# A four-layer GNN kernel: in layer 0, edge features transposed an iteration ahead, and the weighted rows' sums moved

## The chip, the cores and the metric

The kernel runs on one core of one Trainium2 chip, in one launch. The metric is the device time of that launch in microseconds, as the median of several runs. Below, PE is the matrix engine (TensorE), DVE the vector engine, ACT the scalar engine, POOL the GpSimd engine (here it issues the gathers), SP the engine that issues the other DMAs. Each engine works its queue strictly in order, and an instruction that needs another engine's result waits on a semaphore.

## What is computed

Four layers of a graph network over N = 12,500 nodes of 128 values and E = 212,500 directed edges, sorted by their destination. Each layer normalises the node rows, applies a ReLU, sends them through a message step of its own kind, and adds the result to the node rows. The change touches layer 0 alone, an attention layer with edge features (16 values an edge, 4 heads of 32 values), whose reference is

```
Wh = (h @ W.T).reshape(N, H, D)
Wh_src = Wh[src]
Wh_dst = Wh[dst]
attn = (jnp.concatenate([Wh_src, Wh_dst], axis=-1) * a[None]).sum(-1)
attn = jax.nn.leaky_relu(attn, negative_slope=0.2)
attn = attn + edge_feat @ W_e.T
max_v = jax.ops.segment_max(attn, dst, num_segments=N)
...
exp_v = jnp.exp(attn - max_v[dst])
denom = jax.ops.segment_sum(exp_v, dst, num_segments=N)
alpha = exp_v / (denom[dst] + 1e-09)
agg = jax.ops.segment_sum(alpha[..., None] * Wh_src, dst, num_segments=N)
out = agg.reshape(N, H * D)
return _layer_norm(jax.nn.gelu(out, approximate=False), ln_scale, ln_bias)
```

So each edge needs the row of its source node (a gather from device memory), a logit for each head, a softmax over the edges that share a destination, and a sum of the weighted rows for each destination.

## The kernel before

**Tiling.** The edges are cut into NG = 208 groups of 1,024 (T = 8 tiles of 128 edges, one edge a partition). Nodes are worked on in NK = 25 blocks of 512 (`node0`). Since edges are sorted by destination, a group touches only a window of W = 128 destinations, whose place is read from a table into a register. The loop of layer 0 runs over the groups as a software pipeline: in iteration g the logits of group g are made, the softmax of groups of four (SG = 4) follows in steps (`weights`), and the rows of group g - 7 (LAG = 7) are weighted and summed. The transposed sums gather in one large SBUF array, `acc`.

**Order.** The whole block stands under a manual schedule: instructions go into each engine's queue in the order in which the Python code issues them, and the tile framework adds the semaphore waits. A tile has a number of buffers (2 unless `bufs` says otherwise); a new one waits until the last reader of the one that had its place is done.

**One iteration g, in the order of issue.**

- `nodes.step(g)`: one step of each node block under way. A block ends layer 0 for 512 nodes: PE transposes `acc` (L553), ACT a Gelu (L557), DVE norms (L507 to L516, L564 to L566), stores.
- `slots.step(g % 2)`, and again `slots.step()` later: steps of `Slots`, which builds tables for layers 1 and 3 beside this loop (large DVE operations L889 to L971, runs of 20 matmuls L892 and L958).
- `load(g + 2)`: SP issues the loads of `ef` (edge features, 256 KB for four groups, every fourth iteration, 2 buffers), `rb` (256 KB, L1019) and `sdw` (L1023).
- `logits(g)`, first part: POOL issues eight gathers of 128 rows into an X buffer (L730; there are LAG + 8 = 15 X buffers). PE transposes the edge features into the PSUM tile `pt` (L1032, 2 buffers), ACT copies that to `eT` (L1034), PE multiplies it with the edge weights (`pew`, L1036). DVE builds the one-hot `ST` (L1038) and PE multiplies it with `sdw`, eight matmuls (`psd`, L1041). `pew` and `psd` lie in the same tile `pt`.
- `hot(g + 1 - LAG)`: ACT builds the float one-hot S of a later reader (L1102, eight L1105, L1106).
- the second part of `weights`, if one is under way.
- `add_up(g - LAG - 1)`: DVE adds the PSUM tile `pag` (one buffer) to `acc` at the window's place (L1120).
- `spread_out(g - LAG)`: DVE multiplies the gathered rows by alpha into `msg` (L1112, 2 buffers; it is the last reader of X, so that it gives an X buffer back), and PE sums them with eight float32 matmuls, which are 16 instructions, into `pag` (L1116).
- `slots.step()`, the last part of `weights`, and the first part of the next one in every fourth iteration (its loads L1056 and L1058, DVE L1061 to L1074, ACT L1075).
- `logits(g)`, second part: DVE makes `at` from `psd`, X and `pew` (L1044 to L1047), and SP stores it (L1049) for `weights`.

After the loop the last groups are summed in a tail with one `nodes.step` a group.

Of the kernel before, what the change touches and what calls it, by code (L numbers as in the profile page):

```python
# [14 lines left out]
F = mybir.dt.float32  # L15
# [11 lines left out]
P = 128  # L27
T = 8
GE = P * T
W = 128  # L30
H = 4
# [9 lines left out]
LAG = 7  # L41
# [52 lines left out]
def gnn_kernel(ctx: ExitStack, tc, x, src, dst, ef16, ef9, ew, W0, We0, a0, lns, lnb, W1, b1,  # L94
# [6 lines left out]
    NG = NF + (tail > 0)  # L101
# [15 lines left out]
    vec, act, pool, pe = nc.vector, nc.scalar, nc.gpsimd, nc.tensor  # L117
# [36 lines left out]
    def load_rows(t, d, b0, nb):  # L154
        for b, n, r in rows(b0, nb):
            if r < P:
                pool.memset(t[:, b - b0, :], 0.0)
            nc.sync.dma_start(
                t[:r, b - b0 : b - b0 + n, :],
                d[b * P : b * P + (n - 1) * P + r, :].rearrange("(j p) d -> p j d", p=r))  # L160
# [9 lines left out]
    ident = cst.tile([P, P], F, name="ident")  # L170
# [21 lines left out]
    def bcast(v, name):  # L192
# [11 lines left out]
    sp, pp = (pre.enter_context(p) for p in (tc.tile_pool(name="p0", bufs=3),  # L204
                                             tc.tile_pool(name="p0p", bufs=2, space=PSUM)))
# [27 lines left out]
    for k in range(NK):  # L233
# [16 lines left out]
        pt = pp.tile([P, nb, P], F, name="pt")  # L250
# [275 lines left out]
    def cols(k, j=0, n=NBK):  # L526

        c = k * NBK * P if acc.ring is None else k * NBK * P % acc.ring
        return slice(c + j * P, c + min(j + n, NB - k * NBK) * P)

    def settle(k):

        if acc.ring is not None and k and k * NBK * P % acc.ring == 0:
            a = acc.t
            vec.tensor_tensor(a[..., :W], a[..., :W], a[..., acc.ring :], ALU.add)
            vec.memset(a[..., acc.ring :], 0.0)
# [9 lines left out]
    def node0(sp, pp, k):  # L546
        b0, nb = k * NBK, min(NBK, NB - k * NBK)
        xv = sp.tile([P, nb, D], F, name="xv")
        load_rows(xv, x, b0, nb)
        settle(k)  # L550
        pa = pp.tile([P, nb, P], F, name="pa")
        for j in range(nb):
            pe.transpose(pa[:, j, :], acc.t[:, cols(k, j, 1)], ident)  # L553
        yield
        vec.memset(acc.t[:, cols(k)], 0.0)
        o = sp.tile([P, nb, D], F, name="o")
        act.activation(o, pa, AF.Gelu)  # L557
        yield
        for n in norm(sp, o, nb, None):
            if n is None:  # L560
                yield
            else:
                o = n
        vec.tensor_tensor(o, o, lns_b[:, None, :].to_broadcast([P, nb, D]), ALU.mult)  # L564
        vec.tensor_tensor(o, o, lnb_b[:, None, :].to_broadcast([P, nb, D]), ALU.add)
        vec.tensor_tensor(xv, xv, o, ALU.add)  # L566
        yield from keep(sp, 0, k, xv)
# [424 lines left out]
    with (tc.tile_pool(name="e0", bufs=2) as sp, tc.tile_pool(name="e0p", bufs=2, space=PSUM) as pp,  # L992
# [16 lines left out]
        vec.memset(cut_s[:, :, L:], 0.0)  # L1009
        flat = lambda t: t.rearrange("p h k -> p (h k)")  # L1010
        breg, areg = Window(SP, True), Window(DVE, True)
        loads, xs, alphas, hots = {}, {}, {}, {}
        feats = feature_stream(ef16f, 16, 4, "ef", sp)

        def load(g):

            e = feats(g)
            rb = sp.tile([P, T, P], B16, name="rb", bufs=3)
            nc.sync.dma_start(rb.rearrange("p t q -> p (t q)"),  # L1019
                              rel16[g * T : (g + 1) * T, :].rearrange("t q -> (t q)")[None, :].to_broadcast([P, GE]))  # L1020
            sdw = sp.tile([P, 3 * H], B16, name="sdw", bufs=4)
            n0 = breg.load(bi[0:1, g : g + 1])
            breg.end(nc.sync.dma_start(sdw, sdt[ds(n0, W), :]))  # L1023
            loads[g] = e, rb, sdw

        def logits(g):

            e, rb, sdw = loads.pop(g)
            X = xs[g] = sp.tile([P, T, P + H], F, name="X", bufs=LAG + 8)
            gather(X, tab0, si[:, g, :])  # L1030
            pt = pp.tile([P, P + T * H + T * 3 * H], F, name="pt")
            pe.transpose(pt[:, :P], e, ident)  # L1032
            eT = sp.tile([P, P], F, name="eT")
            act.copy(eT, pt[:, :P])  # L1034
            pew = pt[:, P : P + T * H]
            pe.matmul(pew, eT, WeB, start=True, stop=True)  # L1036
            ST = sp.tile([P, T, P], B16, name="ST")
            vec.tensor_scalar(ST, rb, pcol, None, op0=ALU.is_equal)  # L1038
            psd = pt[:, P + T * H :].rearrange("p (t k h) -> p t k h", k=3, h=H)
            for t in range(T):  # L1040
                pe.matmul(psd[:, t].rearrange("p k h -> p (k h)"), ST[:, t, :], sdw, start=True, stop=True)  # L1041
            yield
            at = sp.tile([P, T, H], F, name="at")
            vec.tensor_reduce(at, psd.rearrange("p t k h -> p t h k"), AX.X, ALU.add)  # L1044
            vec.tensor_tensor(at, at, X[:, :, P:], ALU.add)
            vec.scalar_tensor_tensor(at, at, 0.2, at, op0=ALU.mult, op1=ALU.max)
            vec.tensor_tensor(at, at, pew.rearrange("p (t h) -> p t h", h=H), ALU.add)  # L1047
            a0_ = PADF + g * GE
            nc.sync.dma_start(lgt[a0_ : a0_ + GE, :].rearrange("(p t) h -> p t h", t=T), at)  # L1049
# [49 lines left out]
        def hot(g):  # L1099

            far = sp.tile([P, T], F, name="far")
            act.mul(far, rel[:, g, :], -1.0)  # L1102
            S = hots[g] = sp.tile([P, T, W], F, name="oh")
            for t in range(T):
                act.activation(S[:, t, :], iop, AF.Abs, bias=far[:, t : t + 1])  # L1105
            act.activation(S, S, AF.Relu, bias=ones[:, :1], scale=-1.0)  # L1106

        def spread_out(g):

            X, ev, S = xs.pop(g), alphas.pop(g), hots.pop(g)  # L1110
            msg = sp.tile([P, T, P], F, name="msg")
            vec.tensor_tensor(msg.rearrange("p t (h d) -> p t h d", h=H),  # L1112
                              X[:, :, :P].rearrange("p t (h d) -> p t h d", h=H),
                              ev[:, :, :, None].to_broadcast([P, T, H, HD]), ALU.mult)
            for t in range(T):
                pe.matmul(pag, msg[:, t, :], S[:, t, :], start=t == 0, stop=t == T - 1)  # L1116

        def add_up(g):
            win = ds(areg.load(bir[0:1, g : g + 1], RW - 1), W)
            areg.end(vec.tensor_tensor(acc.t[:, win], acc.t[:, win], pag, ALU.add))  # L1120

        with tc.manual_schedule():
            load(0)
            load(1)
            work = []
            nodes = Nodes(lambda k: node0(ns, np_, k), LAG + 2)
            for g in range(NG + 1):
                nodes.step(g)
                slots.step(g % 2)
                if g + 2 < NG:  # L1130
                    load(g + 2)
                now = None
                if g < NG:
                    now = logits(g)
                    next(now)
                if g + 1 >= LAG:
                    hot(g + 1 - LAG)
                for w in work:
                    next(w)
                if g > LAG:  # L1140
                    add_up(g - LAG - 1)
                if g >= LAG:
                    spread_out(g - LAG)
                slots.step()
                for w in work:
                    next(w, None)
                work = []
                if g and g % SG == 0:
                    work = [weights(g // SG - 1)]
                    next(work[0])  # L1150
                    if g == NG:
                        next(work[0])
                        next(work[0], None)
                        work = [weights(NSG)]
                        next(work[0])
                if now is not None:
                    next(now, None)

            next(work[0])
            for k in range(NG - LAG + 1, NG):  # L1160
                nodes.step(k + LAG)
                if k + 1 < NG:
                    hot(k + 1)
                else:
                    next(work[0], None)
                add_up(k - 1)
                spread_out(k)
            add_up(NG - 1)
            while nodes.step(NG + LAG + 2):
                pass  # L1170
            slots.close()
# [89 lines left out]
    with (tc.tile_pool(name="t1", bufs=1) as tp, tc.tile_pool(name="e1", bufs=3) as sp,  # L1261
# [10 lines left out]
        S, pags, X, here, there = {}, {}, {}, [], []  # L1272
# [5 lines left out]
        with tc.manual_schedule():  # L1278
            g = -1
# [120 lines left out]
    with (tc.tile_pool(name="e2", bufs=3) as sp, tc.tile_pool(name="e2p", bufs=2, space=PSUM) as pp,  # L1400
          tc.tile_pool(name="n2", bufs=2) as ns, tc.tile_pool(name="n2p", bufs=1, space=PSUM) as np_):
        acc.t = sp.tile([P, 3, RW + W], F, name="acc2", bufs=1)
        rows2, mix, _, window2 = layer2(sp, pp, 11, True)
        nodes = Nodes(lambda k: node2(ns, np_, k), 4)
# [6 lines left out]
        with tc.manual_schedule():  # L1411
            vec.memset(acc.t, 0.0)
            mixed[0] = mix(0)
            g = -1
# [121 lines left out]
    with tc.tile_pool(name="l3", bufs=1) as lp:  # L1536
        acc.t, acc.ring = lp.tile([P, AW], F, name="acc3"), None
        stats = lp.tile([P, NK, 6], F, name="stats")
        with (tc.tile_pool(name="t3", bufs=1) as tp, tc.tile_pool(name="e3", bufs=2) as sp,
# [15 lines left out]
            X, S, sums, flat3, going = {}, {}, {}, {}, []  # L1555
# [3 lines left out]
            with tc.manual_schedule():  # L1559
# [4 lines left out]
                g, count, nk, alive = -1, 0, 0, True  # L1564
# [65 lines left out]
    with tc.If(coarse > W - 1):  # L1630
# [154 lines left out]
        with tc.tile_pool(name="es2", bufs=1) as sp, tc.tile_pool(name="es2p", bufs=1, space=PSUM) as pp:  # L1785
            _, _, stream2, window2 = layer2(sp, pp)
# [34 lines left out]
```

## Time and profile before

| | |
|---|---|
| time, median of 12 runs | 9865.54 us (9840.95 to 9888.52) |
| the profiled execution's own time | 9878.95 us |
| its span | 9877.2 us |
| granted clock of PE, mean | 0.708 of full speed |
| PE matmul, busy | 5212.4 us (53%) |
| PE weight loads, busy | 3250.0 us (33%) |
| DVE, busy | 5347.9 us (54%) |
| ACT, busy | 2817.2 us (29%) |
| POOL, busy | 5138.6 us (52%) |
| first L1034 and 208th L1034 (layer 0's loop) | 175.8 and 3303.1 us |
| last L1120 (end of layer 0's tail) | 3361.28 us |

The busy times are those of the whole launch; the span is cut into 40 slices for a course in time, and layer 0's loop covers about the first 13 of them. In the costliest groups of instructions a row reads: line, engine, operation, tile out <- tiles in, count; busy us in all, mean ns of one; then how long the engine stood idle just before such an instruction, and what it was waiting for. "remote" is a release that the trace can't put down to one instruction, "issue" time in which the engine waited for nothing that the profile shows. In the timeline a row reads: start, duration, engine, line, operation, tiles, count, and in brackets the idle time before it. The ends of PE's instructions are modelled, so that a matmul's recorded end and the moment at which another engine gets its result can differ.

From 500 to 3250 us, which is 184 groups, with rows for each shape:

| DVE instruction | busy us, mean ns | idle before it, us |
|---|---|---|
| L1120, addition of `pag` to `acc`, x184 | 52.8, 287 | 251.7 |
| L1044, first instruction of `at`, x184 | 46.3, 252 | 216.2 |
| L1112, `msg`, x184 | 223.4, 1214 | 17.1 |
| L1038, `ST`, x183 | 88.6, 484 | 0.0 |

### The profile page before, as it was taken

To read this page: it belongs to the slowest core of one execution; us is meant where nothing else is said; L and a number is where in the kernel's file an instruction comes from. 1 tells how busy PE (TensorE), PEld (TensorE's weight loads), DVE (VectorE), ACT (ScalarE), POOL (GpSimd) and SP (SyncE) were. 2 spreads that over 40 slices of the span, in tenths; PEclk is the share of its full clock that TensorE was granted. 3 is DMA by queue.
4 is the path that set the end of the run, shared out by engine and by line. 5 is a ranking of instruction groups with operands and counts; after the bars stand their busy time and mean duration, and the time that the engine had idled before them with its cause. 6 is when DMAs were issued, how large, how long until landed. Compare 5 with 4: busy or idle time off the path is not lost. (4 is left out here: it accounts for less than half of the span.)

```text
span 9877.2 us, 105557 instructions
## 1 busy us (share of the span) xinstructions
PE 5212.4 (53%) x33167; PEld 3250.0 (33%) x33168; DVE 5347.9 (54%) x10302; ACT 2817.2 (29%) x7509; POOL 5138.6 (52%) x5434
## 2 busy tenths in 40 slices
PE   2233333333333247778783555555555546666766
PEld 2233333333333225555551333333333321111212
DVE  4466666656666413333343777777777753333333
ACT  2133333333333213333331222222222212333333
POOL 2555555555544265555525555555555535555552
PEclk6555565655655568888886777777777767777777
DMA  7222232222322312222221111111111122222223
GB/s 103 65 74 74 74 75 76 72 72 74 77 72 73 72 54 72 70 73 70 75 56 46 48 54 51 52 51 53 50 51 52 46 87 77 78 78 79 79 78 95
DMA packets 740839, 673.64 MB, mean 68 GB/s; under 512 B 340899, under 2 KB 629014, under 8 KB 740247
## 3 DMA queue, kind: packets, MB, share of 16 engines
q0 software_dynamic: 186624, 382.17, 14.7%
q1 hardware_dynamic: 553643, 284.63, 11.4%
q8 instruction: 263, 4.31, 0.2%
q14 instruction: 309, 2.53, 0.1%
HBM read 603.91 MB, written 63.28 MB: 68 GB/s over the span
## 5 line engine op out<-in xcount | busy, mean ns | idle before, releaser
L730 POOL DMA_INDIRECT X<-tab,si x1664 | 1616.2, 971 | 1451.4 <-DVE msg L1112 677.8
L730 POOL DMA_INDIRECT X<-htab,si x1664 | 1575.7, 947 | 1124.3 <-ACT prods L1350 558.3
L738 POOL DMA_INDIRECT xg<-tab,si x968 | 920.2, 951 | 809.4 <-PE pg L1600 427.9
L738 POOL DMA_INDIRECT X<-htab,si x968 | 937.7, 969 | 697.0 <-PE pag L1309 317.7
L1372 PE MATMUL pag<-prods,oh 128*128 128x352 f32 x3328 | 1244.6, 536 | 0.0
L1116 PE MATMUL pag<-oh,msg 128*128 128x128 f32 x3328 | 721.0, 404 | 328.5 <-DVE msg L1112 283.3
L1372 PEld LDWEIGHTS pag<-prods,oh 128*128 128x128 f32 x3328 | 742.8, 229 | 415.4 <-issue 186.0
L1510 ACT CAST xb<-px 128x384 bf16<-128x384 f32 x1050 | 497.8, 479 | 1147.2 <-PE px L1499 605.6
L1116 PEld LDWEIGHTS pag<-oh,msg 128*128 128x128 f32 x3328 | 668.6, 307 | 343.9 <-DVE msg L1112 286.3
L1337 PE MATMUL py<-mixer,eT 72*128 72x120 f32 x416 | 130.8, 407 | 1212.4 <-ACT eT L1336 1051.5
L1246 ACT ACTIVATE xs<-px,wslot 128x128 f32<-128x128 f32 x1050 | 373.9, 367 | 1223.4 <-PE px L1234 577.6
L1036 PE MATMUL pt<-WeB,eT 128*128 128x32 f32 x416 | 123.2, 387 | 1114.1 <-ACT eT L1034 826.1
L1374 ACT COPY R<-pag 128x352 f32<-128x352 f32 x208 | 94.1, 452 | 1935.0 <-remote 1314.3
L1309 PE MATMUL pag<-oh,X 128*128 128x128 f32 x1936 | 464.3, 331 | 305.0 <-issue 151.0
L1600 PE MATMUL pg<-xg,oh 128*128 128x385 bf16 x968 | 395.9, 420 | 426.1 <-DVE f L1593 351.8
L1234 PE MATMUL px<-tabS,oha 128*32 128x128 f32 x8652 | 529.4, 321 | 165.2 <-ACT xs L1246 88.1
L1215 PE MATMUL pw<-ohb,xs 128*128 128x128 f32 x2100 | 591.6, 369 | 15.9 <-ACT xs L1246 14.1
L745 DVE TENSOR_TENSOR oh<-iop,rel 128x1024 f32<-128x1024 f32 (+1 forms) x321 | 389.5, 1214 | 316.5 <-PE pm L1609 101.6
L1499 PE MATMUL px<-tabS,oha 128*32 128x384 bf16 x4326 | 452.5, 405 | 120.6 <-issue 101.1
L1350 ACT ACTIVATE prods<-X,ef 128x128 f32<-128x128 f32 x1664 | 509.8, 392 | 12.4 <-DMA X<-htab,si 12.0
L1337 PEld LDWEIGHTS py<-mixer,eT 72*128 72x128 f32 x416 | 82.6, 248 | 1273.8 <-ACT eT L1336 1093.2
L1036 PEld LDWEIGHTS pt<-WeB,eT 128*128 128x128 f32 x416 | 96.2, 288 | 1187.3 <-ACT eT L1034 875.4
(463 smaller groups left out, 10053.2 us busy)
## 6 DMA issues: line engine op xcount, KB each, us to landing
lob<-lo SPq DMA_DIRECT2D x252, 224.0 KB
rb<-rel SPq DMA_DIRECT2D x208, 256.0 KB
X<-htab,si POOLq DMA_INDIRECT x2632
X<-tab,si POOLq DMA_INDIRECT x1664
xtab<-xv SPq DMA_DIRECT2D x72, 256.0 KB
xv<-xtab SPq DMA_DIRECT2D x72, 256.0 KB
xg<-tab,si POOLq DMA_INDIRECT x968
lob<-lo SPq DMA_DIRECT2D x84, 160.0 KB
```

The costliest lines, as they stand in the source:

```text
L730: pool.indirect_dma_start(out=t[:, s, :], out_offset=None, in_=table[:, :], in_offset=bass.IndirectOffsetOnAxis(ap=idx[:, s : s + 1], axis=0))
L738: pool.indirect_dma_start(out=ts[-1][:, : table.shape[1]], out_offset=None, in_=table[:, :], in_offset=bass.IndirectOffsetOnAxis(ap=idx[:, ...
L745: vec.tensor_tensor(s, iop[:, None, :].to_broadcast([P, T, W]), r[:, :, None].to_broadcast([P, T, W]), ALU.is_equal)
L1116: pe.matmul(pag, msg[:, t, :], S[:, t, :], start=t == 0, stop=t == T - 1)
L1215: pe.matmul(pw, x, b, start=j == 0, stop=j == NT - 1)
L1234: pe.matmul(px[q * SL : (q + 1) * SL, :], a[:, jj * P + q * SL : jj * P + (q + 1) * SL], tabS[:, blk, :], start=True, stop=True)
L1309: pe.matmul(p, r[t], s[:, t, :], start=t == 0, stop=t == T - 1)
L1350: act.activation(A[:, t, :], X[:, t, :], AF.Copy, scale=e[:, t, 0:1])
L1372: pe.matmul(pag, S[:, t, :], prods[:, t, :], start=t == 0, stop=t == T - 1)
L1499: pe.matmul(px[q * SL : (q + 1) * SL, :], a[:, jj * P + q * SL : jj * P + (q + 1) * SL], tabS[:, blk, :], start=True, stop=True)
L1510: act.copy(x[:, : 3 * P], px)
L1600: pe.matmul(p, s[:, t, :], r[t], start=t == 0, stop=t == T - 1)
```

## The change

- The transpose of the edge features and the copy to `eT` leave `logits` and become `turn`, issued for group g + 1 right after the first part of `logits`(g); `turn(0)` stands ahead of the loop. The pair (`pt`, `eT`) is handed on.
- `spread_out` is split: `weigh` holds the product `msg`, `spread_out` the matmuls. `weigh`(g - LAG) stays where `spread_out` stood. `spread_out` now runs an iteration later, on group g - LAG - 1, at the head of the iteration, ahead of the node and slot steps.
- `add_up` runs two iterations after the product, on group g - LAG - 2, and is the first thing that an iteration issues.
- `hot` is built for group g - LAG where it was g + 1 - LAG: an iteration later, as its reader is.
- The tail starts a group earlier, has the new order, and makes two node steps a group where there was one.

```diff
@@ -1009,7 +1009,7 @@
         vec.memset(cut_s[:, :, L:], 0.0)
         flat = lambda t: t.rearrange("p h k -> p (h k)")
         breg, areg = Window(SP, True), Window(DVE, True)
-        loads, xs, alphas, hots = {}, {}, {}, {}
+        loads, feat, turned, xs, alphas, hots, msgs = {}, {}, {}, {}, {}, {}, {}
         feats = feature_stream(ef16f, 16, 4, "ef", sp)
 
         def load(g):
@@ -1021,17 +1021,22 @@
             sdw = sp.tile([P, 3 * H], B16, name="sdw", bufs=4)
             n0 = breg.load(bi[0:1, g : g + 1])
             breg.end(nc.sync.dma_start(sdw, sdt[ds(n0, W), :]))
-            loads[g] = e, rb, sdw
+            feat[g], loads[g] = e, (rb, sdw)
+
+        def turn(g):
+
+            pt = pp.tile([P, P + T * H + T * 3 * H], F, name="pt")
+            pe.transpose(pt[:, :P], feat.pop(g), ident)
+            eT = sp.tile([P, P], F, name="eT")
+            act.copy(eT, pt[:, :P])
+            turned[g] = pt, eT
 
         def logits(g):
 
-            e, rb, sdw = loads.pop(g)
+            rb, sdw = loads.pop(g)
             X = xs[g] = sp.tile([P, T, P + H], F, name="X", bufs=LAG + 8)
             gather(X, tab0, si[:, g, :])
-            pt = pp.tile([P, P + T * H + T * 3 * H], F, name="pt")
-            pe.transpose(pt[:, :P], e, ident)
-            eT = sp.tile([P, P], F, name="eT")
-            act.copy(eT, pt[:, :P])
+            pt, eT = turned.pop(g)
             pew = pt[:, P : P + T * H]
             pe.matmul(pew, eT, WeB, start=True, stop=True)
             ST = sp.tile([P, T, P], B16, name="ST")
@@ -1105,13 +1110,17 @@
                 act.activation(S[:, t, :], iop, AF.Abs, bias=far[:, t : t + 1])
             act.activation(S, S, AF.Relu, bias=ones[:, :1], scale=-1.0)
 
-        def spread_out(g):
-
-            X, ev, S = xs.pop(g), alphas.pop(g), hots.pop(g)
-            msg = sp.tile([P, T, P], F, name="msg")
+        def weigh(g):
+
+            X, ev = xs.pop(g), alphas.pop(g)
+            msg = msgs[g] = sp.tile([P, T, P], F, name="msg")
             vec.tensor_tensor(msg.rearrange("p t (h d) -> p t h d", h=H),
                               X[:, :, :P].rearrange("p t (h d) -> p t h d", h=H),
                               ev[:, :, :, None].to_broadcast([P, T, H, HD]), ALU.mult)
+
+        def spread_out(g):
+
+            msg, S = msgs.pop(g), hots.pop(g)
             for t in range(T):
                 pe.matmul(pag, msg[:, t, :], S[:, t, :], start=t == 0, stop=t == T - 1)
 
@@ -1124,7 +1133,12 @@
             load(1)
             work = []
             nodes = Nodes(lambda k: node0(ns, np_, k), LAG + 2)
+            turn(0)
             for g in range(NG + 1):
+                if g > LAG + 1:
+                    add_up(g - LAG - 2)
+                if g > LAG:
+                    spread_out(g - LAG - 1)
                 nodes.step(g)
                 slots.step(g % 2)
                 if g + 2 < NG:
@@ -1133,14 +1147,14 @@
                 if g < NG:
                     now = logits(g)
                     next(now)
-                if g + 1 >= LAG:
-                    hot(g + 1 - LAG)
+                    if g + 1 < NG:
+                        turn(g + 1)
+                if g >= LAG:
+                    hot(g - LAG)
                 for w in work:
                     next(w)
-                if g > LAG:
-                    add_up(g - LAG - 1)
                 if g >= LAG:
-                    spread_out(g - LAG)
+                    weigh(g - LAG)
                 slots.step()
                 for w in work:
                     next(w, None)
@@ -1157,14 +1171,16 @@
                     next(now, None)
 
             next(work[0])
-            for k in range(NG - LAG + 1, NG):
-                nodes.step(k + LAG)
+            for k in range(NG - LAG, NG):
+                add_up(k - 1)
+                spread_out(k)
                 if k + 1 < NG:
                     hot(k + 1)
-                else:
-                    next(work[0], None)
-                add_up(k - 1)
-                spread_out(k)
+                    if k + 2 == NG:
+                        next(work[0], None)
+                    weigh(k + 1)
+                for _ in range(2):
+                    nodes.step(k + LAG + 1)
             add_up(NG - 1)
             while nodes.step(NG + LAG + 2):
                 pass
```

## The prediction

> **What bounds the kernel now.** I read the page first, for where the time lies. The change touches only the loop of layer 0: its first L1034 starts at 175.8 us and its 208th at 3303.1, so a group of 1024 edges takes (3303.1 - 175.8) / 207 = 15.1 us. No engine is full there (first 13 of the 40 slices):
>
> ```profile
> PE   2233333333333247778783555555555546666766
> DVE  4466666656666413333343777777777753333333
> POOL 2555555555544265555525555555555535555552
> L1116 PE MATMUL pag<-oh,msg 128*128 128x128 f32 x3328 | 721.0, 404 | 328.5 <-DVE msg L1112 283.3
> ```
>
> The windows by 250 us say the same of the middle of the layer (columns: span, then busy time of PE, weight loads, DVE, ACT, POOL, the granted clock, DMA share, GB/s):
>
> ```profile
> 1750.00:2000.00 250.00, 90.45 (x603) 82.94 (x604) 147.90 (x334) 77.75 (x211) 134.53 (x138) 0.62 0.31 76
> ```
>
> DVE is busy 59%, or 8.9 us of a group's 15.1. The eight gathers of a group follow each other every 1.25 us (0.95 and a pause of 0.30), which makes 10.0 us. So a third of the time goes to waits, and the waits of 500 to 3250 us (184 groups) say for what:
>
> ```profile
> PE pt L1036 <- ACT eT L1034: 732.8, 112, 55.5
> POOL X L730 <- DVE msg L1112: 673.0, 71, 25.7
> DVE acc L1120 <- remote: 172.8, 24, 18.3
> DVE at L1044 <- remote: 121.7, 23, 7.4
> DVE acc L1120 <- PE pag L1116: 29.8, 21, 2.1
> ```
>
> POOL stands still until DVE's `msg` gives an X buffer back. DVE stands in front of `msg` because `add_up` waits for PE. PE's 732.8 us for `eT` look like the largest item, but the timeline shows what they are:
>
> ```profile
> 1755.49 3.78 PE L1116 MATMUL pag<-oh,msg 128*128 128x128 f32 x16
> 1759.06 0.35 PE L1032 MATMUL pt<-ident,ef 128*128 128x128 f32 x1
> 1769.42 0.95 POOL L730 DMA_INDIRECT X<-tab,si  x1 [0.30 <-issue]
> 1773.27 0.29 DVE L1120 TENSOR_TENSOR acc<-acc,pag 128x128 f32 x1 [15.54 <-remote]
> 1773.31 0.27 ACT L1034 COPY eT<-pt 128x128 f32<-128x128 f32 x1 [15.10 <-remote]
> 1773.48 1.22 DVE L1112 TENSOR_TENSOR msg<-X,alp 128x1024 f32<-128x1024 f32 x1
> 1773.62 0.63 PE L1036 MATMUL pt<-WeB,eT 128*128 128x32 f32 x2 [14.21 <-ACT eT L1034]
> 1774.96 0.95 POOL L730 DMA_INDIRECT X<-tab,si  x1 [4.60 <-DVE msg L1112]
> ```
>
> The spread matmuls are recorded as over at 1759.27. DVE gets their answer at 1773.27, 2.9 us after POOL's row of gathers ended at 1770.37, and ACT gets the transpose at the same moment. The 15 us are one late answer of PE, seen by three engines; an earlier transpose doesn't remove it. Then comes `msg`, POOL starts again, and the next row of gathers begins.
>
> A page speaks against this reading. The Trainium skill ("SBUF — State Buffer", "Who interferes with whom") states that PE and ACT wait on nobody and that DMA shares no port with an engine; by it the 2.9 us after the gathers would be chance. The row 1773.27 shows the two together, without showing why.
>
> **The change, part by part.** No instruction and no DMA is added or removed; everything is a matter of order, one more turn of the tail aside.
>
> *Transposes an iteration ahead.* Each group's L1032 and L1034 are moved behind the psd matmuls of the group before. What they can free is the gap between L1034's end and L1036, 0.35 us in PE's rows (0.65 in the weight loads' one), hence at most 0.65 x 206 = 134 us. It is covered today by DVE's `add_up` and `msg`, for which the spread behind it waits (328.5 us idle in front of L1116): 0.29 + 1.22 us against 0.27 of transpose, 0.27 of copy and the gap. I take 0, and keep -134 as the bound. If that cover went, the 0.35 would stand in the chain below. The moved step needs its `ef` a round earlier. The load stays where it was, behind the `lgt` store in SP's queue (1751.57 and 1751.94), so its lead falls from two rounds to one, and one round is 5.3 us at its shortest. The nearest row is `d`, loaded with no lead: DVE waited for it 97.5 us in 15 of 46 cases, 6.5 us each. Once in four groups, 52 x 15/46 x (6.5 - 5.3) = +20 us is the upper end, the lower is 0; I take 0, being nearest to a load with a lead. If it is late, PE stands at L1032 and the next spread behind it.
>
> *The sums an iteration later, the addition two later.* Order on PE becomes spread(g-8), pew(g), psd(g), transpose(g+1); on DVE add_up(g-9), node and slot steps, ST(g), msg(g-7), slot and softmax steps, at(g). Here lies the cost. Four instructions of `at` (L1044 to L1047) wait for psd(g), which now stands behind 16 spread matmuls. Behind `at` in DVE's queue stands add_up of the next iteration, which frees `pag`, the only buffer of its kind, for the next spread; behind that stand ST and the next `msg`, for which POOL waits. So a closed chain runs through every iteration:
>
> ```profile
> 1844.11 0.25 DVE L1044 TENSOR_REDUCE at<-pt 128x32 f32<-128x96 f32 x1
> 1846.58 0.28 DVE L1120 TENSOR_TENSOR acc<-acc,pag 128x128 f32 x1
> 1846.78 1.21 DVE L1112 TENSOR_TENSOR msg<-X,alp 128x1024 f32<-128x1024 f32 x1
> 1847.14 0.41 PE L1036 MATMUL pt<-WeB,eT 128*128 128x32 f32 x2 [2.31 <-ACT eT L1034]
> 1847.39 0.35 PE L1041 MATMUL pt<-sdw,ST 128*128 128x12 bf16 x8
> 1848.05 3.62 PE L1116 MATMUL pag<-oh,msg 128*128 128x128 f32 x16 [0.31 <-DVE msg L1112]
> ```
>
> The chain before is spread, add_up, msg: 3.62 + 0.20 (until msg starts) + 1.21 + two hand-offs of 0.05 = 5.13 us; in the slower place, from the spread at 1750.20 to that at 1755.49, it is 5.29. After, it is spread, pew and psd, at, add_up: 3.62 + 0.60 (1847.14 to 1847.74) + 0.92 (1844.11 to 1845.03) + 0.28 + four hand-offs of 0.05 = 5.62; with the slower place's rows 3.78 + 0.84 (1754.76 to 1755.60) + 1.07 (1756.27 to 1757.34) + 0.29 + 0.20 = 6.18. So +0.49 to +0.89 us a round, 0.69 in the middle. It costs where DVE waits for PE: L1120's 24 + 21 waits and L1044's 23 make at least 68 of 184 groups, 37%; at most all. Over 206 rounds: least 0.49 x 206 x 0.37 = +37, most 0.89 x 206 = +183, middle 0.69 x 206 x 0.69 = **+97 us**.
>
> A second way to the same term: when a row of gathers ends and PE's late answer comes, before it was followed by add_up and msg at once. Now psd (0.60), at (0.92) and the next ST (0.48) lie between, 2.0 us. POOL had 71 waits for `msg`, 80 over 208 groups: 160 us if all are of that kind, 54 if only the 27 (24 scaled) with a late L1120 are; middle 107.
>
> The rule on matmuls in the Trainium skill ("Perfetto Trace Analysis", "Matmuls") speaks against the change as well: independent groups of matmuls should rotate through PSUM banks, so that emptying one overlaps the next group. With one `pag`, emptied behind `at`, nothing overlaps; an estimate by it, with 0.92 + 0.28 us in the open in each of 206 rounds, is +247.
>
> *Hot, msg and the buffers.* `hot` is issued an iteration later, and so is its reader: 0. `msg` stays in its iteration, so X comes free where it did; the second `msg` buffer covers the round that it now waits. On SP's queue nothing changes place: the load of g+2 still stands between `at`(g-1)'s store and `at`(g)'s.
>
> *The tail.* A round there takes 3.62 us (L1120 at 3350.47 and 3354.09), set by msg and spread and also by ACT, whose `hot` is 0.2 + 2.18 + 1.15. One more round: +3.6; two node steps a round bring the node work forward, which ends with two blocks after 3361: -4 at most. Sum 0.
>
> *Sum.* 0 + 97 + 0 = +97. On the profiled execution, 9878.95 us (a span of 9877.2 and 1.75 around it), that is 9976. It lies 13.4 us above the median of the 12 runs, and the change's time will be such a median: 9865.5 + 97 = 9962, or **9960**.
>
> **Rivals.** *Faster: the slack frees X earlier (30%).* `msg`(g-7) no longer stands behind the sums of g-8, only behind those of g-9. If psd(g) is out whenever DVE gets to `at`(g), L1120's waits vanish with nothing in their place: (172.8 + 29.8) x 208/184 = 229 us at most, 115 if half. For it: DVE has 8.9 - 0.92 - 0.28 = 7.7 us of other work a round, against 4.2 of spread and psd. Against: that work comes in lumps, and late answers are 15 us. It decides from the point where PE answers in under 7.7 us. Half: 9865.5 - 115 = 9750; all: 9636.
>
> *No change (8%).* DVE's and POOL's own work sets the pauses and both chains hide under it, 5.6 against 7.7 us: 9865, 20 us to either side. Against: DVE did wait 252 us in front of L1120. Nor is it out of the question that the order changes while the late answers don't: the change would do what it says and the sum of DVE's waits would stay at L1044.
>
> *Slower (62%)* is the forecast; its own range is 9,890 to 10,070 (+37 less 12 of scatter; +183 and the 20 of `ef`).
>
> **How the numbers follow.** A difference below 0.2%, 20 us, can't be told from none here. The range must take in most of the faster case: from 9720, beyond the half gain by 30, to 10070. Outside are gains above 145 us (about 12%) and losses above 205 (about 7%).
>
> **What would show it.** Right: L1120's 251.7 us of idle time (all causes) fall below 60, L1044's 216.2 rise above 400, L1036 no longer waits for `eT`, POOL's waits for `msg` grow, and a group takes 15.5 us or more. The `ef` term: a DMA in front of L1032. Wrong: L1044's wait stays near 216 while L1120's falls, and POOL's waits shrink. If layers 1 to 3 move, it is something that I left out.

## The result, and the profile after

The changed kernel takes 10169.12 us (median of 8 runs, 10124.39 to 10183.32) against 9871.21 us for the kernel before (34 runs): a ratio of 1.0297, with a 95% interval of 1.0285 to 1.031. It is 298 us slower. The forecast was slower, but at 9960 us, and the range ended at 10070.

The loss lies where the change is. The profiled execution's span grew by 10157.3 - 9877.2 = 280 us, and from layer 1's first gather on it is the same (6486 before, 6481 us after). The copies of `eT` (L1034, now L1031) run from 172.1 to 3579.1 us: 16.46 us a group in place of 15.11, which is 280 us over 207 steps. From the last gather of layer 0 to layer 1's first one it is 168 us in place of 162.

The page after, with the same rows and the first 14 slices to be read:

```profile
PE   2133333333333325778786355555555554677666
DVE  4355556555565532333334477777777762333333
POOL 3444445444454335555552555555555535555553
L1125 PE MATMUL pag<-oh,msg 128*128 128x128 f32 x3328 | 752.8, 417 | 1730.0 <-DVE acc L1129 662.9
```

All three engines are emptier. PE stands 1730 us in front of the spread matmuls where it stood 328, but most of that has only moved: its 1114.1 us in front of L1036 are 59.0 in front of the same matmul, now L1041. The window from 1750 us (same columns as before) has fewer of everything, 115 gathers in place of 138:

```profile
1750.00:2000.00 250.00, 74.31 (x508) 69.90 (x507) 130.32 (x281) 63.64 (x173) 108.59 (x115) 0.58 0.24 62
```

The waits from 500 to 3250 us, now 169 or 170 groups:

```profile
ACT eT L1031 <- remote: 1026.9, 72, 23.2
POOL X L730 <- DVE msg L1117: 828.8, 73, 29.1
PE pag L1125 <- ACT oh L1111: 582.0, 46, 22.8
PE pag L1125 <- DVE acc L1129: 543.6, 57, 26.1
DVE at L1049 <- remote: 306.9, 43, 14.8
DVE acc L1129 <- issue: 105.2, 170, 1.0
```

POOL waits longer for `msg`. PE's spread now waits for `hot` (ACT's L1111), a wait that the rows of before don't have. DVE's groups in the same stretch, first of after, then of before:

```profile
L945 DVE TENSOR_TENSOR ohr<-iop,r 128x2560 bf16<-128x2560 f32 x34 | 95.9, 2821 | 101.8 <-ACT oh L1110 76.0 <-issue 25.7
L889 DVE TENSOR_TENSOR ohb<-iop,bk 128x1960 bf16<-128x1960 f32 x36 | 78.8, 2189 | 82.8 <-issue 45.0 <-ACT oh L1110 37.8
L1129 DVE TENSOR_TENSOR acc<-acc,pag 128x128 f32 x170 | 49.1, 289 | 105.2 <-issue 105.2
L1049 DVE TENSOR_REDUCE at<-pt 128x32 f32<-128x96 f32 x170 | 42.8, 252 | 328.7 <-remote 306.9 <-issue 12.2 <-PE pq L958 6.9
```

```profile
L945 DVE TENSOR_TENSOR ohr<-iop,r 128x2560 bf16<-128x2560 f32 x38 | 106.9, 2814 | 14.7 <-issue 8.1 <-ACT oh L1105 6.1
L889 DVE TENSOR_TENSOR ohb<-iop,bk 128x1960 bf16<-128x1960 f32 x38 | 83.2, 2190 | 8.2 <-issue 7.1 <-ACT oh L1105 1.0
```

The addition's wait for PE is gone: of its 251.7 us, 202.6 were labelled "remote" or with PE's spread, and the 105.2 us that it has now are all "issue". `at` has taken it over (216.2 to 328.7). These two cancel: a group has 0.75 us less of the one and 0.76 us more of the other. What is new is in the two upper rows: L945 and L889 are DVE operations of the slot tables for layers 1 and 3, which the change doesn't touch, and they wait for ACT's one-hot. Over all 42 + 42 of them in the layer, the view of each line adds up to 241 us of idle time after and 26 before. Of the 241 us, 152 are labelled with ACT's L1110 and 89 "issue"; in both traces all 42 L945 and 39 of the 42 L889 carry a wait on the semaphore that ACT raises. How that looks in the timeline:

```profile
1875.53 0.31 PE L1029 MATMUL pt<-ident,ef 128*128 128x128 f32 x1
1885.15 0.95 POOL L730 DMA_INDIRECT X<-tab,si  x1 [0.30 <-issue]
1889.15 0.27 ACT L1031 COPY eT<-pt 128x128 f32<-128x128 f32 x1 [16.94 <-remote]
1889.56 2.18 ACT L1110 ACTIVATE oh<-iop,far 128x128 f32<-128x128 f32 x8
1891.77 2.83 DVE L945 TENSOR_TENSOR ohr<-iop,r 128x2560 bf16<-128x2560 f32 x1 [19.30 <-ACT oh L1110]
...
1899.94 0.25 DVE L1049 TENSOR_REDUCE at<-pt 128x32 f32<-128x96 f32 x1
...
1901.47 0.29 DVE L1129 TENSOR_TENSOR acc<-acc,pag 128x128 f32 x1 [0.61 <-issue]
1901.90 0.55 PE L1125 MATMUL pag<-oh,msg 128*128 128x128 f32 x1 [26.06 <-DVE acc L1129]
```

The transpose of the next group's features stands behind spread and `psd` on PE, and its answer is late: it comes 3 us after the row of gathers that ended at 1886.10. ACT's queue has the copy, then `hot`. DVE's slot step starts when `hot`'s eight L1110 are done, 0.03 us behind them; most of its 19.30 us of idle time is PE's late answer, handed on by the copy and `hot`. Behind it in DVE's queue stand `at` and `add_up`, for which PE's next spread waits. L945 and L1110 share one operand: both read `iop`, the row of numbers 0 to 127, which lines 177 and 178 put into PSUM.

### The profile page after: what moved, and what is told of

Same layout as the page of the kernel before. It is cut to its first block, busy times and chain, and to the rows that moved or that the text cites. A ratio compares the mean times of both kernels' runs of the same rounds, so it can differ in the third digit from the quotient of the medians.

```text
span 10157.3 us, 105742 instructions
## 1 busy us (share of the span) xinstructions
PE 5173.4 (51%) x33167; PEld 3260.5 (32%) x33168; DVE 5344.6 (53%) x10302; ACT 2821.3 (28%) x7511; POOL 5129.6 (51%) x5434
## 5 line engine op out<-in xcount | busy, mean ns | idle before, releaser
L1125 PE MATMUL pag<-oh,msg 128*128 128x128 f32 x3328 | 752.8, 417 | 1730.0 <-DVE acc L1129 662.9
L1125 PEld LDWEIGHTS pag<-oh,msg 128*128 128x128 f32 x3328 | 703.1, 321 | 1822.2 <-issue 1032.8
L1031 ACT COPY eT<-pt 128x128 f32<-128x128 f32 x208 | 55.3, 266 | 2079.4 <-remote 1289.3
L1396 DVE TENSOR_TENSOR acc<-acc,pT 128x384 f32 x208 | 114.5, 550 | 680.7 <-remote 602.1
```

## The experiments

Each set of kernels ran on one chip beside the kernel before, and the chips differ: the kernel before takes 9790 to 9871 us on those of the result and of the second set, 7369 to 7382 us on the others, so each ratio is to the kernel before of its own set. Three theories were put to the test. **C** is the prediction's: the ring spread, psd, at, add_up, spread. **H**: the spread waits for `hot`, which stands behind the copy of `eT`. **R**, which came up after the second set: DVE's slot steps wait for `hot`, because of the PSUM tile that both read.

### One order at a time

*e1: `hot` ahead of the copy.* The changed kernel, with

```diff
-                    if g + 1 < NG:
-                        turn(g + 1)
                 if g >= LAG:
                     hot(g - LAG)
+                if g + 1 < NG:
+                    turn(g + 1)
```

> The kernel after, with one swap: hot(g - LAG) is issued ahead of turn(g + 1), so that on ACT the one-hot of the next spread no longer stands behind the copy of eT. Theory H: the loss is the ring spread, pew and psd, transpose, copy of eT, hot, spread, 3.6 + 0.7 + 0.35 + 0.27 + 3.55 = 8.5 us of work with a late answer of PE in it; with the swap hot leaves the ring, and most of the 298 us goes: 0 to 80 us over the kernel before. Theory C (the prediction's ring spread, psd, at, add_up, mis-sized): hot is not in it, so the time stays at +250 to +300.

Measured: 7458.32 against 7381.26 us, 1.010 (1.0083 to 1.0117), +77 us. Run twice more (below), 1.0102 and 1.011.

*e2: the spread behind psd.* `spread_out(g - LAG - 1)` moved from the head of the iteration to between `logits` and `turn`.

```diff
-                if g > LAG:
-                    spread_out(g - LAG - 1)
                 nodes.step(g)
...
                     next(now)
-                    if g + 1 < NG:
-                        turn(g + 1)
+                if g > LAG:
+                    spread_out(g - LAG - 1)
+                if g + 1 < NG:
+                    turn(g + 1)
```

> The kernel after, with spread_out moved from the head of the iteration to behind the psd matmuls, ahead of the next transpose. Theory C: psd(g) no longer stands behind the 16 spread matmuls, at and add_up get out of the ring, and most of the 298 us goes: 0 to 80 us over before. Theory H: the ring spread, transpose, copy, hot, spread stays closed (7.8 of 8.5 us), so +200 to +300 stays.

Measured: 7665.09 us, 1.0387 (1.037 to 1.0405), +284 us. Theory C expected the loss to go, and it is the largest of all. The idle time of L889 and L945 is 243 us in this run, 20 in e1.

*e3: the transposes ahead, alone.* The kernel before with `turn` as in the change, all else in its old place.

```diff
+            turn(0)
             for g in range(NG + 1):
...
                     next(now)
+                    if g + 1 < NG:
+                        turn(g + 1)
                 if g + 1 >= LAG:
                     hot(g + 1 - LAG)
```

> The kernel before, with only the transposes and the copies of eT turned an iteration ahead; sums, addition, hot and tail as before. Prediction's step: 0, with the bound of -134 us and up to +20 for the edge features' load. Theory H: hot(g - 6) is issued an iteration ahead of its reader, so the copy ahead of it does little: within 40 us of before. Theory C: within 40 us too. If this alone costs 150 or more, both theories miss the cause.

Measured: 7408.52 us, 1.0037 (1.0023 to 1.0051), +27 us. The bound of a gain, 134 us, isn't touched. L889 and L945 idle 60 us.

*e4: the sums moved, alone.* The changed kernel with `turn(g)` called inside `logits(g)`.

```diff
+            turn(g)
             pt, eT = turned.pop(g)
...
-            turn(0)
...
-                    if g + 1 < NG:
-                        turn(g + 1)
```

> The kernel after, with the transposes and the copy back in logits of their own group; spread, add_up, hot and tail as after. Theory H: copy and hot stand one behind the other here too, the copy's transpose behind the spread, and hot's reader is the next spread: +200 to +330 over before. Theory C as the prediction sized it: +37 to +183, middle 97.

Measured: 7586.45 us, 1.0273 (1.0256 to 1.029), +205 us, and 136 us of idle time at L889 and L945. So the sums' move brings most of the loss, by way of `hot` or of what waits for it.

### Hot alone, and the two rings

*The change itself again.*

> The changed kernel itself, beside the others of this set. The first four experiments ran where the kernel before takes 7381 us instead of 9866, with no late answers of PE in the trace; this run gives the change's own ratio beside its variants. If the cost is the ring through hot and not the late answers, +200 to +300 us there too (ratio 1.027 to 1.04); if it is the late answers, less than 1.01 where there are none.

Measured: 10062.89 against 9790.32 us, 1.0287 (1.027 to 1.0304), +273 us. This set's chip is one of the slower ones.

*e5: `hot` ahead of the copy and the spread behind psd.*

```diff
-                if g > LAG:
-                    spread_out(g - LAG - 1)
                 nodes.step(g)
...
                     next(now)
-                    if g + 1 < NG:
-                        turn(g + 1)
+                if g > LAG:
+                    spread_out(g - LAG - 1)
                 if g >= LAG:
                     hot(g - LAG)
+                if g + 1 < NG:
+                    turn(g + 1)
```

> The kernel after, with hot ahead of the copy of eT (as in the first experiment) and the spread matmuls behind psd (as in the second). Theory H + C (hot's ring is most of the loss, psd behind the spread the rest of 77 us): the rest goes too, 0 to 40 us over before, or up to 60 under it. If the 77 us that were left are something else (tail, the transposes ahead: 27 us measured alone), it stays at 50 to 80 over before.

Measured: 9856.34 us, 1.0069 (1.0052 to 1.0086), +66 us. Against e2 only the place of `hot` differs; the wait of L889 and L945 is 23 us. The expectation of 0 to 40 was missed: with the addition first in the iteration, DVE now waits for the spread itself (the addition's waits labelled remote are 436.5 us in 500 to 3250).

*e6: `hot` ahead and two sums in PSUM.* e1, with `pag` as one tile of two halves used in turn.

```diff
-        pag = pp.tile([P, W], F, name="pag", bufs=1)
+        pag = pp.tile([P, 2, W], F, name="pag", bufs=1)
...
-                pe.matmul(pag, msg[:, t, :], S[:, t, :], start=t == 0, stop=t == T - 1)
+                pe.matmul(pag[:, g % 2, :], msg[:, t, :], S[:, t, :], start=t == 0, stop=t == T - 1)
...
-            areg.end(vec.tensor_tensor(acc.t[:, win], acc.t[:, win], pag, ALU.add))
+            areg.end(vec.tensor_tensor(acc.t[:, win], acc.t[:, win], pag[:, g % 2, :], ALU.add))
```

> The first experiment's kernel with two PSUM buffers for the sums, pag, so that a spread no longer waits for the addition of the group before. Theory C: what was left, 77 us, is the spread waiting for add_up behind at: it falls to 40 us or less. If psd behind the spread is what costs (at waits for psd), the second buffer changes little, and 60 to 80 us stay.

Measured: 9863.01 us, 1.0076 (1.0058 to 1.0093), +73 us. It didn't do what it was meant to: PE's spread still waits for the addition (588.4 us, 63 times). So this is e1 on a slower chip, and says nothing on the second buffer.

*e8: `hot` late, alone.* The kernel before with `hot(g - LAG)` in place of `hot(g + 1 - LAG)`, and `hot(k)` in the tail.

```diff
-                if g + 1 >= LAG:
-                    hot(g + 1 - LAG)
+                if g >= LAG:
+                    hot(g - LAG)
...
-                if k + 1 < NG:
-                    hot(k + 1)
-                else:
+                hot(k)
+                if k + 1 == NG:
```

> The kernel before with one thing changed: hot is built for group g - LAG, in the iteration of its own spread, behind that iteration's copy of eT; sums, addition and transposes stay where they were. Theory H: this alone closes the ring spread, transpose, copy, hot, spread, so it costs as much as the whole change or more: +150 to +350 us. Theory C, and the prediction's zero for hot: within 40 us of before.

Measured: 9822.1 us, 1.0036 (1.0024 to 1.0049), +32 us. Theory H expected 150 to 350: the ring through `hot` is closed here (PE's spread waits 220.6 us for it from 500 to 3250 us), but it is not what the change costs. What e8 leaves out is the wait of the slot steps: 41 us at L889 and L945 in place of 26. That sent me to theory R, and to the semaphores: all 42 L945 wait on the one that ACT raises, in the kernel before too; there, DVE came to them behind `add_up`(g - 8), which waits for the same spread anyway.

### The shared PSUM tile

The edit is one operand. `io` holds the same numbers in SBUF.

```diff
-                act.activation(S[:, t, :], iop, AF.Abs, bias=far[:, t : t + 1])
+                act.activation(S[:, t, :], io, AF.Abs, bias=far[:, t : t + 1])
```

*e9: the changed kernel with it.*

> The kernel after, with one operand changed: hot reads the row of numbers 0 to 127 from SBUF (io) and no longer from the PSUM tile iop, which DVE's slot steps (L889, L945, L948) read too. Theory R (the trace's semaphores: each of these DVE steps waits for the hot issued before it, since both read the same PSUM tile, and hot stands behind the copy of eT, the transpose, psd and the spread): the wait goes, DVE's idle time in front of L889 and L945 (184.6 us in 170 groups, about 226 in all, against some 26 before) with it, and the kernel comes to 40 to 120 us over before. Theory H (the spread waits for hot): untouched, +230 to +300 stays.

*e10: the kernel before with it.*

> The kernel before, with hot reading io from SBUF in place of iop. Theory R: before, the slot steps hardly waited for hot (14.7 and 8.2 us idle), so within 30 us of before, as far as ACT is no slower at reading SBUF. Theory H: the same. A gain of more than 40 us would say that ACT's own waits for the slot steps (26.5 us) hold something up.

*e12: the changed kernel with it, and `hot` ahead of the copy.*

> Both edits on the kernel after: hot ahead of the copy of eT, and hot reading io. If R and H are two prices, this is below each of the single edits; if R alone is the price, it equals the run with io alone within 20 us. Theory C (psd and at behind the spread) leaves +40 to +80 over before in any case.

*e1 again.*

> The first experiment's kernel (hot ahead of the copy of eT) beside these: R and H both expect +40 to +110 over before, as the copy no longer stands ahead of hot, so that hot is done before either of its two waiters asks.

Measured against 7368.8 us: e9 7454.37, 1.0109 (1.0086 to 1.0132), +86; e12 7426.76, 1.0076 (1.0053 to 1.0099), +58; e1 7450.93, 1.0102 (1.0074 to 1.013), +82; e10 7355.8, 0.9983 (0.9967 to 0.9999), -13. The changed kernel had not run on such a chip, so the set was repeated with it:

> The changed kernel beside its variants. On a chip where before takes 9800 us: 1.027 to 1.031 as twice before. On one where it takes 7370: theories R and H need no late answers of PE, so a loss of 180 to 300 us (1.024 to 1.041) is expected there too; if it stays under 1.012, the loss needs the late answers.

> The changed kernel with hot reading io. Theory R as the larger price: at least 100 us below the changed kernel of this set, DVE's idle time in front of L889 and L945 under 40 us; H as the larger price: less than 60 us below it.

> The changed kernel with hot ahead of the copy of eT. R and H: 40 to 110 us over before, so 150 us or more below the changed kernel of this set; what it lies below the run with io alone is H's price.

> The kernel before with hot reading io: 0.996 to 1.000 as measured once; on a chip with late answers of PE within 0.5% to either side, since the rows of before show only 23 us of waits of the slot steps and 26.5 us of ACT's.

Measured against 7380.97 us: the changed kernel 7606.75, 1.0304 (1.0285 to 1.0322), +226; e9 7474.51, 1.0124 (1.0105 to 1.0143), +94; e1 7458.78, 1.011 (1.0093 to 1.0127), +78; e10 7368.26, 0.9986 (0.9976 to 0.9995), -13. One operand takes 132 of the 226 us away; 13 us it also saves in the kernel before. It isn't a shorter one-hot that does it: an L1110 takes 387 ns with `io` in e9 and 383 ns with `iop` in the changed kernel. DVE's two groups from 500 to 2300 us, first in the changed kernel, then in e9:

```profile
L945 DVE TENSOR_TENSOR ohr<-iop,r 128x2560 bf16<-128x2560 f32 x30 | 84.6, 2819 | 72.4 <-ACT oh L1110 72.4
L889 DVE TENSOR_TENSOR ohb<-iop,bk 128x1960 bf16<-128x1960 f32 x33 | 72.2, 2187 | 57.2 <-ACT oh L1110 57.2
```

```profile
L945 DVE TENSOR_TENSOR ohr<-iop,r 128x2560 bf16<-128x2560 f32 x33 | 92.7, 2808 | 0.0
L889 DVE TENSOR_TENSOR ohb<-iop,bk 128x1960 bf16<-128x1960 f32 x34 | 74.3, 2184 | 0.0
```

The waits are not shortened but gone, and in e9's trace neither line carries a wait on ACT's semaphore any more, so the shared tile made them. PE still waits for `hot` in e9 (183.2 us in the run of the first of these two sets), and taking that out as well, in e12 of the same set, gave 28 us more (7454.37 to 7426.76): H's price.

Over the runs on the faster chips, the loss follows this one idle time, with 41 to 94 us on top wherever the sums are moved (the kernel before left no trace on such a chip; e10 stands for it):

| kernel | L889 and L945 idle, us | over before, us |
|---|---|---|
| e10, before with io | 0 | -13 |
| e3, transposes ahead alone | 60 | +27 |
| e12, hot ahead, io | 0 | +58 |
| e1, hot ahead (three runs) | 20 | +77, +82, +78 |
| e9, io (two runs) | 0 | +86, +94 |
| e4, sums moved alone | 136 | +205 |
| the change | 170 | +226 |
| e2, spread behind psd | 243 | +284 |

### What is left

*e13: e12 with the two halves of `pag`.*

> The changed kernel with hot ahead of the copy, hot reading io, and two PSUM buffers for the sums. Theory C (the spread waiting for add_up is what is left): 20 us or less over before where the run without the second buffer had 58. If DVE's 0.6 us in front of add_up, the tail (9 us) and the rest are what is left: 40 to 70 over before as without it.

Measured: 7444.97 against 7382.25 us, 1.0081 (1.0065 to 1.0096), +63 us, as e12. PE's group of spreads from 500 to 2300 us, in e12 and then in e13:

```profile
L1125 PE MATMUL pag<-oh,msg 128*128 128x128 f32 x2624 | 575.7, 409 | 761.0 <-DVE acc L1129 516.6 <-DVE rs L513 191.4 <-DVE bI L862 29.3
```

```profile
L1125 PE MATMUL pag<-oh,msg 128*128 128x128 f32 x2608 | 579.2, 412 | 754.4 <-DVE acc L1129 511.4 <-DVE rs L513 190.8 <-DVE bI L862 28.6
```

The wait for the addition is as long as it was: a second half of one PSUM tile doesn't take it away, so this theory wasn't tried by the run, and what a second tile would bring stays open. What can be read instead is DVE, summed in front of each instruction from the 21st to the 201st copy of `eT`: in e12 that stretch is 57 us longer than in e10 of the same set, and so is DVE's idle time: 28 in front of the addition, 14 of `msg`, 10 of `at`, 7 of L894, less 2 in the rest. The addition's is of this kind:

```profile
L1129 DVE TENSOR_TENSOR acc<-acc,pag 128x128 f32 x165 | 47.7, 289 | 101.9 <-issue 101.9
L1117 DVE TENSOR_TENSOR msg<-X,alp 128x1024 f32<-128x1024 f32 x164 | 198.2, 1208 | 26.8 <-ACT alp L1100 26.7
```

Each addition loses 0.6 us in which nothing is waited for that the profile shows (in e10 such waits of the addition are 30.7 us in all); that it is the load of the window's register, now first in the iteration with nothing ahead of it, wasn't tried.

*e15: the version that the runs point to.* The kernel before with io, and 16 X buffers in place of 15.

```diff
-            X = xs[g] = sp.tile([P, T, P + H], F, name="X", bufs=LAG + 8)
+            X = xs[g] = sp.tile([P, T, P + H], F, name="X", bufs=LAG + 9)
...
-                act.activation(S[:, t, :], iop, AF.Abs, bias=far[:, t : t + 1])
+                act.activation(S[:, t, :], io, AF.Abs, bias=far[:, t : t + 1])
```

> The kernel before with hot reading io and 16 X buffers in place of 15. Where gathers run nearly without pause (POOL 385 us of pauses, 0.3 each): within 15 us of the run with io alone, 0.998 to 1.000. Where POOL stands for msg (673 us of waits in 184 groups): the gathers' rows can become one group longer, which gains a pause or lengthens PE's late answers, 0.99 to 1.01.

Measured: 7372.87 us, 0.9987 (0.9978 to 0.9996), the same as e10's 0.9986 without the buffer. The kernel before with `io` in `hot` is 0.14 and 0.17% faster than the kernel before in its two sets; the intervals end just below 1, and the gain is less than the 0.2% that the prediction held to be the least that can be told. It had no run on a chip of the slower kind.

## Why the prediction was wrong

The sign and the layer were right; the size was a third, 97 of 298 us. Most of the loss comes from a wait that the prediction had put at nothing, so that it forecast a loss was right in good part by luck.

**The step that failed** is "*Hot, msg and the buffers.* `hot` is issued an iteration later, and so is its reader: 0." The wait of `hot`'s own reader costs little: e8, which delays `hot` alone, 32 us, and by the step from e9 to e12 28. But an instruction's followers are not only those that read what it writes. DVE's slot steps wait for `hot` since both read the PSUM tile `iop`; `hot` had come to stand behind a copy that waits for spread, psd and transpose; and `at`, `add_up` and the next spread stand behind the slot steps. On the faster chip the price is 132 of 226 us, by one operand. On the slower chips this operand wasn't tried alone. There the same 84 instructions idle 215 us more in the change than before, and the runs with `hot` ahead of the copy, which have hardly any of that wait (23 and 18 us), lie at 1.0069 and 1.0076 (e5, e6) where the change lies at 1.0287; but they take H's wait out with it. The prediction did follow waits to what is queued behind them on the engine; it looked only for waits on data and on buffers that come free, not for one between two readers. The rows that would have shown it were there: L945 and L889 had "ACT oh L1105" as a releaser in the trace of before, with 7.9 and 1.0 us.

**The chain that was priced**, +97 (37 to 183), has its waits where the prediction put them, but not its price. The addition's wait for PE vanished and `at` took it over: 251.7 to 105.2, and 216.2 to 328.7, where below 60 and above 400 were named. The exchange is even. With `hot` out of the way, all that the moved sums and transposes cost is 58 and 63 us (e12, e13), and 66 and 73 on the slower chip (e5, e6). That lies inside the range of the term, but it isn't shown to be this chain: in e12 DVE's rows put 10 us to `at` and 28 to a pause in front of the addition that the term doesn't hold, and e5, which takes `psd` from behind the spread, is hardly better than e6, which doesn't. The rule on rotating PSUM banks in the Trainium skill ("Perfetto Trace Analysis", "Matmuls"), by which the prediction had an estimate of +247, came near to the measured loss by a sum that the runs don't bear out: `pag` stayed single in e12 at +58.

**The transposes ahead**, 0: alone +27 us, again with the slot steps' wait (60 us of idle time). There was no gain, as predicted, but e3 ran on a chip without late answers, so it doesn't test the reason given for it; in the change the copies' waits labelled "remote" did stay (673.4 us before, 1026.9 after). L1041 hardly waits for `eT` any more, as predicted, and it is worth nothing. The `ef` term (up to +20) didn't show: the transpose waits for that load once, 14.6 us, as it did before, 14.3.

**The tail**, 0: +5 us from the last gather to the next layer.

**The second way to the sum** (54 to 160, middle 107) agreed with the first because both left out the same thing; two sums over one chain are not two witnesses.

**The rivals.** Faster: `msg` did get free of the sums of g - 8, but POOL's wait for it grew, 673.0 us in 184 groups to 828.8 in 169. No change: on the faster chips `at` idles only 10 us more, so that DVE's other work does seem to hide most of the priced chain, the argument of that rival; it can't hide the wait of the slot steps, which lies inside that work.

## What to carry to other kernels

When an instruction is moved in one engine's queue, list who waits for its engine's semaphore at all, and not only who reads its result: two engines that merely read the same PSUM tile were kept in program order here (whether an SBUF tile read by both would be, wasn't tried). A constant that several engines read is better given to each from its own place; the edit is one operand. And a new place in a queue is judged by the instruction ahead of it: `hot` was cheap where it stood, and became dear behind a copy that waits for the end of PE's round.

## What the runs showed of the hardware

In these runs the late answers of PE went with the chip and not with the program. On the faster chips the gathers run on with hardly a pause (POOL's idle time in e10 is nearly all the 0.3 us between two gathers), and the same changed kernel has no "remote" wait at `at`, where the other chip had 306.9 us. From 500 to 2300 us there:

```profile
L1049 DVE TENSOR_REDUCE at<-pt 128x32 f32<-128x96 f32 x152 | 37.9, 250 | 11.7 <-PE pt L1046 6.8 <-issue 4.4
```

A group of the changed kernel takes 11.67 us on that chip and 16.46 on the other, and the rest of the launch, from layer 1's first gather on, 4932 and 6481 us, while the gathers (0.95 us each) and DVE's operations are equally long on both, and PE's granted clock in the layer nearly the same (0.59 and 0.58 from 1750 to 2000 us). So the prediction's reading, that a row of gathers holds PE's answers back, was a description of one kind of chip: gathers in a row are not enough for it. What makes a chip answer late stays open. The change cost nearly the same share on both kinds of chip, 1.0297 and 1.0287 on the slower, 1.0304 on the faster.
